# A scheme of 33 products for the last output stage of a cross-attention kernel

## The chip, the cores and the metric

The kernel runs on one core of a Trainium2 chip. Its engines work side by side, each on its own queue of instructions: PE (TensorE, matrix products), DVE (VectorE), ACT (ScalarE), POOL (GpSimd) and SP (SyncE, which here issues the transfers). They wait for each other on semaphores. The metric is the time of one execution on the device in microseconds (us); it is the median of several runs.

## The reference

Two batches of 2048 tokens with 640 channels attend, with 20 heads of 32 channels, to two short contexts of 77 tokens each (a text and an image prompt), which have their own softmax. Everything is in float32. Cut to what matters:

```
q = heads(x @ Wq.T)
k, v = heads(text @ Wk.T), heads(text @ Wv.T)
k_ip, v_ip = heads(ip @ Wk_ip.T), heads(ip @ Wv_ip.T)
out = softmax(q k^T / sqrt(32)) v + softmax(q k_ip^T / sqrt(32)) v_ip
return out @ Wo.T + bo + x
```

The change lies in the last line, for the second batch: a 640x640 matrix times 640x2048 attention outputs, plus a bias and the residual x.

## The kernel before, in words

All matrices lie with the channels on the 128 partitions, so 640 channels are five chunks (`NC = 5`). A step `u` is one chunk of four heads for half of a batch's tokens (1024): there are 20 steps. A step makes queries (PE, line 221), scores (L253), takes them out of the PSUM banks (ACT, L265), forms maxima, differences, exponentials, sums and quotients (DVE L274 and L292, POOL L279 and L299, ACT L285), transposes the result (DVE L306) and multiplies it with the values (PE L315); ACT copies the attention output into `aT` (L338 and L342). The order in which each engine's queue holds these pieces is written out by hand, step by step, in the table `ORDERS`; the output products of the first batch are put between the pieces of steps 10 to 19 (`OUTPUT`).

The output is formed for token blocks of 512. For the first four channel chunks, inputs and outputs both, a block is a 2x2 matrix of blocks (two pairs of chunks, two halves of 256 tokens), and seven products stand for the eight that it needs (Strassen's scheme in Winograd's form). `sum_t` forms differences of token blocks on POOL (L414), `sum_w` differences of weights (L384, once, on POOL), `product` runs on PE (L481 over the first four chunks, L491 for the fifth one, which rides along in four of the seven products), and `take_product` adds the banks to the residual on DVE (L506 with the bias, L512 without). The fifth output chunk is a plain product, `last_chunk` (L461), taken by `store_last` (L471).

For the second batch the four token blocks are done in a tail, after the loop. Near the end of the loop (step 19) SP loads the residual tokens from HBM again: `begin` issues three pieces of the last chunk and the first block (L844 to L848), and after the loop come the last piece and three more blocks. Then stand the 16 differences on POOL, and the list of 28 products and four last chunks in the order in which PE takes them. Inside a block a product writes a bank, is added to the residual, and joins the next product's sum in the same bank where the scheme shares it (`JOINS`). Finished parts are stored at once.

What the tail reads: `aT` (attention outputs), `wo` (Wo, within the tile `wo_ct`), the differences of weights in the fourth x tile, `xs[3]`. The differences of tokens lie in the first three x tiles and in `pb`, the tile that held the probabilities; the residual lies in `pb`, `acc` and `res`.

Of the kernel before, what the change touches and what calls it, by code (L numbers as in the profile page):

```python
# [1 line left out]

# [8 lines left out]
ALU = mybir.AluOpType  # L11
AX = mybir.AxisListType

B, S, C, CC, LT = 2, 2048, 640, 1024, 154
H, D, TEXT = 20, 32, 77
# [4 lines left out]
def kernel(  # L20
# [25 lines left out]
    nc = tc.nc  # L46
    P = 128
    NC = C // P
    NCC = CC // P
    G = P // D  # L50
    TB = 512
    NH = 2
    BLK = NH * TB
    NT = BLK // P
    SUB = S // BLK
    NHB = SUB * NH
    GROUPS = ((0, 3), (3, 3), (6, 2))
    L = TEXT
    assert TEXT == IP and SUB == 2
    NK = (2 * L + D - 1) // D  # L60
    LP = NK * D
    SCALE = 1.0 / float(D) ** 0.5
    NP = B * NC
    NU = NP * SUB
    OPEN = 4
# [7 lines left out]
    banks = [psum.tile([P, TB], F32, name=f"bank_{n}") for n in range(2 * G)]  # L73
    halves = banks[:G], banks[G:]
    wqs = [const.tile([P, NC, P], F32, name=f"wq_{n}") for n in range(3)]
    bo_sb = const.tile([P, NC], F32, name="bo_sb")
    kT = const.tile([P, NC, B, 2, L], F32, name="kT")
    v4s = [const.tile([P, G, NK, D], F32, name=f"v4_{n}") for n in range(2)]
    xs = [const.tile([P, NC, TB], F32, name=f"x_{n}") for n in range(NHB)]
    aT = const.tile([P, (NC + 1) * NHB, TB], F32, name="aT")  # L80

    acc = const.tile([P, NC - 1, TB], F32, name="acc")
    res = const.tile([P, TB], F32, name="res")
# [11 lines left out]
    wo = wo_ct.rearrange("p (k o) -> p k o", k=NC)  # L95
# [95 lines left out]
    XROOM = NHB - 1  # L191
# [131 lines left out]
    def rows_of_attention(b, c):  # L323


        if b == 0:
            return aT[:, ts(c + 1, NHB)]
        if c == 0:
            return aT[:, ts(0, NHB)]
        return aT[:, NHB + c - 1 : NHB + NHB * NHB : NHB]  # L330
# [23 lines left out]
    a11, a12, a21, a22 = wide[:, 0, 0], wide[:, 1, 0], wide[:, 0, 1], wide[:, 1, 1]  # L354
# [31 lines left out]
    def block(b, i, r, h):  # L386

        m, n = (
            4 * (k + 1) + i if b == 0 else 4 * i + k + 3 if k else i for k in (r, r + 2)
        )  # L390
        return aT[:, m : n + 1 : n - m, ts(h, HT)]

    pb_flat = pb.rearrange("p z n g l -> p (z n g l)")
    pb_tiles = pb_flat.rearrange("p (n t) -> p n t", t=TB)

    def t_of(m, b, i):


        raw = {1: (0, 0), 2: (1, 0), 3: (1, 1)}
        if m in raw:  # L400
            return block(b, i, *raw[m])
        if b == 0:
            return t1_room if m == 5 else block(b, i, *{6: (0, 0), 7: (0, 1), 4: (1, 0)}[m])
        sums = pb_tiles[:, : NC - 1] if i == XROOM else xs[i][:, : NC - 1]
        return sums[:, (5, 7, 6, 4).index(m)].rearrange("p (kp t) -> p kp t", kp=2)

    def sum_t(m, b, i):
        x, y = {
            5: (block(b, i, 0, 1), block(b, i, 0, 0)),
            7: (block(b, i, 1, 1), block(b, i, 0, 1)),  # L410
            6: (block(b, i, 1, 1), t_of(5, b, i)),
            4: (block(b, i, 1, 0), t_of(6, b, i)),
        }[m]
        nc.gpsimd.tensor_tensor(t_of(m, b, i), x, y, ALU.subtract)  # L414
# [5 lines left out]
    def sums_of(b, i):  # L420
        if b == 0 or i == 1:
            return acc
        return pb_tiles[:, ds((NC - 1) * (i + 1), NC - 1)]

    def last_of(b, i):
        return res if b == 0 or i == XROOM else xs[i][:, NC - 1]

    def part_in(t, s, h):
        return t.rearrange("p (op s) (h t) -> p s h op t", s=2, h=2)[:, s, h]
# [6 lines left out]
    def in_dram_last(t, b, i):  # L436
        return t[ts(NC - 1, P), ds(b * S + i * TB, TB)]
# [21 lines left out]
    def last_chunk(ps, b, i, ks):  # L459
        for k in ks:  # L460
            nc.tensor.matmul(  # L461
                ps,
                wo[:, k, ts(NC - 1, P)],
                rows_of_attention(b, k)[:, i],
                start=(k == 0),
                stop=(k == NC - 1),
            )

    def store_last(ps, b, i):
        t = last_of(b, i)  # L470
        nc.vector.scalar_tensor_tensor(t, ps, bo_sb[:, NC - 1 :], t, ALU.add, ALU.add)  # L471
        store(b, i, "last")

    def product(m, b, i, ps):


        fifth = {2: (0, 0), 5: (1, 1), 3: (None, 1), 4: (1, 0)}.get(m)
        for op in range(2):
            part = ps[:, ts(op, HT)]
            for kp in range(2):  # L480
                nc.tensor.matmul(  # L481
                    part,
                    w_of[m][:, kp, op],
                    t_of(m, b, i)[:, kp],
                    start=(op == kp == 0 and m in (1, 2, 5)),
                    stop=(op == 1 and kp == 1 and not fifth),
                    skip_group_check=True,
                )
            if fifth:
                s, h = fifth  # L490
                nc.tensor.matmul(  # L491
                    part,
                    w_last[:, op] if s is None else wo[:, NC - 1, ts(2 * op + s, P)],
                    rows_of_attention(b, NC - 1)[:, i, ts(h, HT)],
                    start=False,
                    stop=(op == 1),
                    skip_group_check=True,
                )

    def take_product(m, b, i, ps):  # L500
        part = {2: (0, 0), 1: (0, 0), 5: (1, 1), 7: (1, 1), 3: (0, 1), 6: (0, 1), 4: (1, 0)}[m]
        t = part_in(sums_of(b, i), *part)
        if m in (5, 3, 4, 1 if b else 2):
            for op in range(2):
                bias = bo_sb[:, ds(2 * op + part[0], 1)]
                nc.vector.scalar_tensor_tensor(  # L506
                    t[:, op], ps[:, ts(op, HT)], bias, t[:, op], ALU.add, ALU.add
                )
                if b and m == 4:
                    nc.sync.dma_start(out=in_dram(outT, b, i, *part)[:, op], in_=t[:, op])  # L510
        else:
            nc.vector.tensor_tensor(t, t, ps.rearrange("p (op t) -> p op t", op=2), ALU.add)  # L512
        if m in (6, 7, 2 if b else 1) or m == 4 and not b:
            store(b, i, part)
# [11 lines left out]
    for k in (0, half):  # L526
        nc.sync.dma_start(
            out=wo_ct[:, ds(k * B * LT, half * B * LT)].rearrange("p (k n) -> p k n", k=half),
            in_=ctxT[ds(k * P, half * P), :].rearrange("(k p) n -> p k n", p=P),
# [16 lines left out]
    for t in range(2):  # L546

        ps = halves[t][G - 2 + t]
# [176 lines left out]
    for u in range(NU + 1):  # L725
        for e, text in enumerate(ORDERS[kind_of(u)][2:]):
            for t in text.split():
                m = u - 1 if t[-1] == "-" else u
                t = t.strip("-")
                if t[0] == "C" and t != "CA":  # L730
                    w = work[(m, int(t[1:]))][0]
# [18 lines left out]
    for t, u in queues[3]:  # L750
        if t[0] == "G":
            m = (None, 5, 6, 7, 4)[int(t[1])]
            i = sum(1 for x in sums_at if x[0] == m)
            sums_at[(m, i)] = (t, u)
            work[(t, u)] = (m, i)
    JOINS = {3: 5, 6: 1, 7: 6, 4: 7}
    for t, u in queues[0]:
        if t[0] == "F":
            n = int(t[1:])
            w = work[(u, n)]  # L760
# [15 lines left out]
    late = [c for c in chunks if c[0] >= SUB * NC]  # L776
    for e in range(4):
        for t, u in queues[e]:
            q, b, c, sub = step_of(u)
            ahead = need.setdefault((t, u), [])  # L780
            k, i = t[0], t[1:]
# [20 lines left out]
            elif k == "C":  # L802
                w = work[(u, int(i))]
                ahead += [("F" + i, u)]
                if w[0] == "q":
                    n = chunks.index(w[1:]) - 5
                    if n >= 0:
                        m, h = chunks[n]
# [3 lines left out]
            elif k == "F":  # L812
                w = work[(u, int(i))]
# [11 lines left out]
            elif k == "G":  # L825
                m, n = work[(t, u)]
# [11 lines left out]
    def begin(u):  # L838

        q, _, _, sub = step_of(u)  # L840
        load_w()
        if sub == 1 and q + 3 < NP:
            load_wq(q + 3)
        if u == NU - 1:  # L844

            for i in range(OPEN - 1):
                nc.sync.dma_start(out=last_of(1, i), in_=in_dram_last(xT, 1, i))
            fetch_sums(0)  # L848

    def fetch_sums(i):  # L850
        nc.sync.dma_start(
            out=sums_of(1, i),
            in_=xT[: (NC - 1) * P, ds(S + i * TB, TB)].rearrange("(o p) t -> p o t", p=P),
        )

    def emit(t, u):
        q, b, c, sub = step_of(u)
# [51 lines left out]
    while any(queues):  # L909
# [4 lines left out]
                written.add(queue.pop(0))  # L914
                moved = True
        assert moved, [queue[:1] for queue in queues]
    nc.sync.dma_start(out=last_of(1, XROOM), in_=in_dram_last(xT, 1, XROOM))
    for i in range(1, NHB):
        fetch_sums(i)
    for i in range(NHB):  # L920
        for m in (5, 7, 6, 4):
            sum_t(m, 1, i)
    ends = [held[("p", i)] for i in range(OPEN)]
    free = [p for p in banks if all(p is not t for t in ends)] + ends
    at = {}
    for m, i in (
        (1, 0), ("o", 0), ("o", 1), ("o", 2), ("o", 3), (2, 0), (5, 0), (1, 1), (2, 1), (5, 1),
        (3, 0), (6, 0), (3, 1), (6, 1), (7, 0), (1, 2), (7, 1), (2, 2), (4, 0), (5, 2), (4, 1),
        (1, 3), (2, 3), (5, 3), (3, 2), (6, 2), (3, 3), (6, 3), (7, 2), (7, 3), (4, 2), (4, 3),
    ):  # L930
        if m == "o":
            last_chunk(ends[i], 1, i, (NC - 1,))
            store_last(ends[i], 1, i)
            continue
        at[(m, i)] = at.pop((JOINS[m], i)) if m in JOINS else free.pop(0)
        product(m, 1, i, at[(m, i)])
        take_product(m, 1, i, at[(m, i)])
        if m in (2, 3, 4):
            free.append(at.pop((m, i)))


# [1 line left out]
_TOKENS = ("x", "ctx_2048")  # L943
# [28 lines left out]
```

## Time and profile before

| what | us |
|---|---|
| median of 3 runs | 508.86 (508.68 to 509.0) |
| span of the profiled execution | 506.7 |
| between that span and the median of the runs | 2.16 |
| busy in the span: PE | 498.3 (98%) |
| busy in the span: DVE | 391.9 (77%) |
| busy in the span: POOL | 395.0 (78%) |
| busy in the span: ACT | 242.5 (48%) |
| the tail's first product on PE starts | 437.12 |
| its last DVE instruction ends | 503.88 |

The page gives a span for the profiled execution, from its first instruction to its last; the time of a run is longer by what lies around it. The table's difference is taken between that span and the median. Engines overlap, so their busy times do not add up to the span. In a group of instructions "128x512" is partitions by elements, and the mean is the duration of one instruction. A matrix product in float32 leaves two records on PE. In the order of time, a bracket gives the idle time ahead of an instruction and what ended it.

### The profile page before, as it was taken

What the parts mean: (1) busy time and instruction counts of PE and PEld (TensorE: products, weight loads), DVE (VectorE), ACT (ScalarE), POOL (GpSimd) and SP (SyncE); (2) the same over time, 40 slices, a digit from 0 to 9 for tenths busy, and PEclk for the clock granted to TensorE, in tenths of its full rate; (3) what the DMA queues carried; (4) which work ended last, traced back from release to release, by engine and by line L of the source; (5) the groups of instructions that cost most, each with busy time, mean ns of one, the idle gap of its engine ahead of it and who ended that gap; (6) DMA issues with size and microseconds to landing.
All of it is one profiled execution on the core that took longest, in us unless ns stands there. A gap on an engine that the chain in (4) does not pass through costs nothing.

```text
span 506.7 us, 10153 instructions
## 1 busy us (share of the span) xinstructions
PE 498.3 (98%) x4270; PEld 321.0 (63%) x4270; DVE 391.9 (77%) x347; ACT 242.5 (48%) x423; POOL 395.0 (78%) x163
## 2 busy tenths in 40 slices
PE   9999999999999999999999999999999999999997
PEld 5657557557656565456565656554755775588885
DVE  0079999999899987958997997699899999333333
ACT  1266666666676566645545636454654750100000
POOL 0079999989989988899999997798899999940000
PEclk9999999999999999999999999999999999999999
DMA  8982621331362453885574485168323242641213
GB/s 274 357 210 61 159 69 46 86 92 46 92 185 74 112 198 116 284 314 145 159 237 124 131 260 158 53 178 292 110 72 95 86 162 65 225 147 62 84 41 104
DMA packets 71053, 73.03 MB, mean 144 GB/s; under 512 B 5600, under 2 KB 50912, under 8 KB 71008
## 3 DMA queue, kind: packets, MB, share of 16 engines
q1 hardware_dynamic: 70288, 71.67, 45.9%
q8 instruction: 33, 0.54, 0.5%
q10 hardware_dynamic: 720, 0.72, 0.4%
q14 instruction: 12, 0.10, 0.1%
HBM read 58.61 MB, written 10.49 MB: 136 GB/s over the span
## 4 chain that ended last, share of the span: by engine, by line
PE 86%; DMA 5%; POOL 4%; DVE 1%; SPq 1%; issue 1%; ACT 0%; DVEq 0%; POOLq 0%
PE bank L221 31%; PE bank L481 18%; PE bank L253 9%; PE bank L315 9%; PE bank L137 9%; PE bank L461 5%; PE bank L491 5%; DMA x<-in_x_dram 3%; DMA wo_ct<-in_L_xattn_Wo_dram 2%; POOL pb L299 2%; POOL pb L279 1%; SPq L175 1%; POOL x L384 1%; DMA acc<-in_x_dram 1%; PE bank L541 1%
## 5 line engine op out<-in xcount | busy, mean ns | idle before, releaser
L279 POOL TENSOR_TENSOR pb<-pb,mx 128x1848 f32<-128x1848 f32 (+1 forms) x60 | 175.4, 2941 | 45.3 <-DVE mx L274 45.1
L221 PE MATMUL bank<-x,wq 128*128 128x512 f32 x400 | 180.7, 601 | 0.1
L299 POOL TENSOR_TENSOR pb<-pb,rden 128x1848 f32<-128x1848 f32 (+1 forms) x60 | 175.0, 2939 | 5.2 <-DVE rden L294 5.2
L274 DVE TENSOR_REDUCE mx<-pb 128x24 f32<-128x1848 f32 (+1 forms) x60 | 109.6, 1845 | 33.0 <-ACT pb L265 32.8
L265 ACT COPY pb<-bank 128x462 f32<-128x462 f32 (+1 forms) x240 | 101.7, 535 | 59.3 <-PE bank L253 58.5
L221 PEld LDWEIGHTS bank<-x,wq 128*128 128x128 f32 x400 | 74.1, 191 | 85.0 <-issue 81.7
L292 DVE TENSOR_REDUCE den<-pb 128x24 f32<-128x1848 f32 (+1 forms) x60 | 110.4, 1840 | 17.3 <-ACT pb L285 16.9
L285 ACT ACTIVATE pb<-pb 128x1848 f32<-128x1848 f32 (+1 forms) x60 | 94.9, 1582 | 56.4 <-POOL pb L279 56.2
L306 DVE STREAM_TRANSPOSE pb<-pb 128x1920 f32<-128x1920 f32 (+1 forms) x60 | 114.8, 1923 | 2.1 <-POOL pb L299 2.1
L253 PEld LDWEIGHTS bank<-kT,qT 32*128 32x128 f32 x1280 | 47.4, 184 | 26.3 <-issue 18.0
L253 PE MATMUL bank<-kT,qT 32*128 32x154 f32 x1280 | 58.7, 306 | 0.7 <-ACT vT L899 0.4
L315 PE MATMUL bank<-pb,v 32*32 32x512 f32 x1600 | 55.8, 597 | 1.2 <-ACT pb L265 0.7
L481 PE MATMUL bank<-aT,wo_ct 128*128 128x256 f32 x192 | 47.6, 382 | 1.0 <-DVE acc L512 0.7
L137 PEld LDWEIGHTS bank<-wo_ct,aT 128*128 128x128 f32 x320 | 43.1, 188 | 4.2 <-issue 3.5
L315 PEld LDWEIGHTS bank<-pb,v 32*32 32x32 f32 x1600 | 30.7, 103 | 23.2 <-issue 11.8
L137 PE MATMUL bank<-wo_ct,aT 128*128 128x154 f32 x320 | 45.3, 295 | 0.0
L481 PEld LDWEIGHTS bank<-aT,wo_ct 128*128 128x128 f32 x192 | 36.0, 190 | 11.0 <-issue 3.8
L231 ACT COPY qT<-bank 128x512 f32<-128x512 f32 x40 | 23.1, 588 | 31.4 <-PE bank L221 31.4
L461 PE MATMUL bank<-aT,wo_ct 128*128 128x512 f32 x80 | 36.1, 597 | 0.0
L506 DVE SCALAR_TENSOR_TENSOR pb<-bank,bo_sb,pb 128x256 f32<-128x256 f32 x24 | 10.5, 479 | 26.9 <-PE bank L491 16.4
L491 PE MATMUL bank<-aT,wo_ct 128*128 128x256 f32 x96 | 28.6, 379 | 0.0
L506 DVE SCALAR_TENSOR_TENSOR acc<-bank,bo_sb,acc 128x256 f32<-128x256 f32 x40 | 17.0, 466 | 13.3 <-PE bank L491 6.6
(47 smaller groups left out, 286.2 us busy)
## 6 DMA issues: line engine op xcount, KB each, us to landing
x<-in_x_dram SPq DMA_DIRECT2D x20, 1280.0 KB, 6.9
x<-in_x_dram SPq DMA_DIRECT2D x21, 256.0 KB, 5.2
out_dram<-acc SPq DMA_DIRECT2D x19, 256.0 KB, 2.8
acc<-in_x_dram SPq DMA_DIRECT2D x16, 256.0 KB, 6.7
v<-vS SPq DMA_DIRECT2D x160, 20.0 KB, 1.8
pb<-in_x_dram SPq DMA_DIRECT2D x3, 1024.0 KB, 7.6
wq<-in_L_xattn_Wq_dram SPq DMA_DIRECT2D x9, 320.0 KB, 4.8
aT<-in_L_xattn_Wk_dram SPq DMA_DIRECT2D x5, 512.0 KB, 5.6
```

Of the source, the lines that this page charges most:

```text
L137: nc.tensor.matmul(keys_in(out), loaded[n][:, k, :], cT[:, k, :, t, :], start=(k == 0), stop=(k == NCC - 1))
L221: nc.tensor.matmul(pq, wqs[q % 3][:, k, :], xs[place_of(u, h)][:, k, :], start=(k == 0), stop=(k == NC - 1),)
L253: nc.tensor.matmul(ps[g][:, ts(t, 2 * L)], qTs[(u, h)][g * D : (g + 1) * D, ts(st, P)], kT[g * D : (g + 1) * D, c, b].rearrange("p t l -> ...
L265: nc.scalar.copy(keys_of(u, s)[:, :, g], ps[g][:, : n * 2 * L].rearrange("p (n l) -> p n l", n=n))
L274: nc.vector.tensor_reduce(mx, rows_of(u, s), AX.X, ALU.max)
L279: nc.gpsimd.tensor_tensor(rows_of(u, s), rows_of(u, s), maxs[s].unsqueeze(3).to_broadcast([P, n, 2, L]), ALU.subtract)
L285: nc.scalar.activation(e, e, AF.Exp, scale=SCALE)
L292: nc.vector.tensor_reduce(den, rows_of(u, s), AX.X, ALU.add)
L299: nc.gpsimd.tensor_tensor(rows_of(u, s), rows_of(u, s), rdens[s].unsqueeze(3).to_broadcast([P, n, 2, L]), ALU.mult)
L306: nc.vector.transpose(p, p)
L315: nc.tensor.matmul(pa[r][g * D : (g + 1) * D, :], v4s[q % 2][rows, g, k, :], zones[rows, :, g, k, :], start=(k == 0), stop=(k == NK - 1),)
L481: nc.tensor.matmul(part, w_of[m][:, kp, op], t_of(m, b, i)[:, kp], start=(op == kp == 0 and m in (1, 2, 5)), stop=(op == 1 and kp == 1 and ...
```

## The change

The second batch's tail is written anew; the first batch's output and all of the attention stay.

The first four output chunks by all five input chunks are now one 4x5 matrix of 128x128 weight blocks, and the 2048 tokens' attention outputs a 5x2 matrix of blocks with 1024 tokens each. A scheme of 33 products stands for the 40 that this needs. Each product is one block of weights (raw, or a sum) times one block of tokens (raw, or a sum), and runs twice, once for each 512 columns.

- `W_SUMS`: 25 sums of 128x128 weight blocks, 40 instructions on DVE, into `pb`. 37 of them stand in DVE's queue ahead of the first evacuation of a bank.
- `R_SUMS`: 25 sums of token blocks, 128x1024. 20 are on POOL, five (L, G, J, X and P) on DVE, at given places in its queue. They go to `xs[3]`, free parts of `aT` and `pb`, and three of them over attention outputs that nobody needs any more.
- `CHAINS`: the products are added up in eight chains; each chain has one bank for a token half, and after each stage the bank as it then stands is added to or taken from some outputs. That gives 62 additions on DVE, and four for the last output chunk, all 128x512.
- `TAIL` gives the order in which all of these are issued. A later product of a chain waits until DVE has read the bank of the stage before.
- The residuals are no longer loaded again, but for one block: the x tiles still hold the tokens of the last three query blocks, and sums are formed in them in place. The fourth block is loaded after the loop, into `acc` and `res`.
- One of the four parts of Wo (`a21`) was overwritten in the first batch's scheme. Two transfers load it again after the loop, and SP issues them behind the first batch's last store.

The diff, cut to its core:

```diff
         if sub == 1 and q + 3 < NP:
             load_wq(q + 3)
-        if u == NU - 1:
-
-            for i in range(OPEN - 1):
-                nc.sync.dma_start(out=last_of(1, i), in_=in_dram_last(xT, 1, i))
-            fetch_sums(0)
...
-    nc.sync.dma_start(out=last_of(1, XROOM), in_=in_dram_last(xT, 1, XROOM))
-    for i in range(1, NHB):
-        fetch_sums(i)
...
-    for i in range(NHB):
-        for m in (5, 7, 6, 4):
-            sum_t(m, 1, i)
...
-        product(m, 1, i, at[(m, i)])
-        take_product(m, 1, i, at[(m, i)])
...
+    PRODUCTS = (
+        "01 11, 03 Q, K C, M 00, 30 E, B M, L 30, 31 S, W 40, D X, "
...
+    TAIL = (
+        "xpA.0 wG wP wU wQ wV wX wW wC wD wA wI wJ wT wE wO m31.1.0 wH wF m31.0.1 wN wM o2 wK wS m0.0.1 wL q2 "
+        "xpS.1 m25.0.2 t0.0.11 m0.1.0 t6.0.10 m25.1.3 t0.1.11 xpU.2 m7.1.6 t6.1.10 o1 t2.1.21 o3 t2.1.31 "
...
+    for kp in range(2):
+        nc.sync.dma_start(
+            out=a21[:, kp],
+            in_=WoT[ts(2 * kp, P), : (NC - 1) * P].rearrange("p (op s o) -> p s op o", s=2, o=P)[:, 1],
+        )
+    nc.sync.dma_start(
+        out=acc,
+        in_=xT[: (NC - 1) * P, ds(S + fourth * TB, TB)].rearrange("(o p) t -> p o t", p=P),
+    )
+    nc.sync.dma_start(out=res, in_=xT[ts(NC - 1, P), ds(S + fourth * TB, TB)])
...
+    def add_part(o, ps, op):
+        t = sum_at(o)
+        if o in untouched:
+            untouched.discard(o)
+            nc.vector.scalar_tensor_tensor(t, t, bo_sb[:, o[0] : o[0] + 1], ps, ALU.add, op)
+        else:
+            nc.vector.tensor_tensor(t, t, ps, op)
+        parts_left[o] -= 1
+        if not parts_left[o]:
+            m, i = o
+            nc.sync.dma_start(out=outT[ts(m, P), ds(S + i * TB, TB)], in_=t)
...
+    for word in TAIL:
+        k, rest_ = word[0], word[1:]
+        if k == "w":
+            out = weight(rest_)
+            (op, a), *more = terms(W_SUMS[number(rest_)])
...
+            for n, (o2, b) in enumerate(more):
+                if n == 0 and op == ALU.subtract:
+                    nc.vector.scalar_tensor_tensor(out, weight(a), -1.0, weight(b), ALU.mult, o2)
+                else:
+                    nc.vector.tensor_tensor(out, weight(a) if n == 0 else out, weight(b), o2)
+        elif k == "x":
+            e, (w, where) = rest_[0], rest_[1:].split(".")
...
+            (nc.vector if e == "d" else nc.gpsimd).tensor_tensor(places[w], ra, rb, op)
...
+            nc.tensor.matmul(ps, weight(w), tokens_of(x)[:, h], start=first, stop=True, skip_group_check=True)
```

In `TAIL`, w is a sum of weights, xp a token sum on POOL and xd one on DVE, m a product (number, token half, bank), t an addition of a chain's bank to an output, o a last chunk on PE and q its addition.

## The prediction

> **What bounds the kernel now.** I read first the page's busy shares and its 40 slices, to see which engine is never free and where that changes. Columns of the slices: 12.7 us each, busy tenths.
>
> ```profile
> PE 498.3 (98%) x4270; PEld 321.0 (63%) x4270; DVE 391.9 (77%) x347; ACT 242.5 (48%) x423; POOL 395.0 (78%) x163
> ...
> PE   9999999999999999999999999999999999999997
> ...
> DVE  0079999999899987958997997699899999333333
> ...
> POOL 0079999989989988899999997798899999940000
> ```
>
> PE is full to the end. DVE and POOL are nearly full until slice 34; in the last six DVE has two thirds of its time to spare, and from about 449 us POOL has nothing to do. The change lies there. Next the stretches of ten us (columns: engine busy us with instruction counts, granted clock, DMA share, GB/s), and the instructions of PE, POOL and DVE in order of time (start, duration, group).
>
> ```profile
> 420.00:430.00 10.00, 10.00 (x31) 5.62 (x30) 9.93 (x10) 0.37 (x1) 9.97 (x5) 1.00 0.24 76
> 430.00:440.00 10.00, 9.66 (x175) 5.29 (x174) 1.39 (x3) 2.31 (x8) 9.84 (x8) 1.00 0.54 156
> 440.00:450.00 10.00, 10.00 (x42) 7.67 (x41) 5.03 (x10) 0.00 (x0) 8.78 (x8) 1.00 0.79 296
> 450.00:460.00 10.00, 10.00 (x48) 8.81 (x47) 3.54 (x8) 0.00 (x0) 0.00 (x0) 1.00 0.08 26
> ```
> ```profile
> 437.12 1.99 PE L481 MATMUL bank<-aT,wo_ct 128*128 128x256 f32 x8 [0.34 <-ACT aT L342]
> 438.95 3.60 PE L461 MATMUL bank<-aT,wo_ct 128*128 128x512 f32 x8
> 442.38 1.03 PE L481 MATMUL bank<-aT,wo_ct 128*128 128x256 f32 x4
> ...
> 502.38 0.59 PE L491 MATMUL bank<-aT,wo_ct 128*128 128x256 f32 x2
> ```
> ```profile
> 427.04 3.56 DVE L306 STREAM_TRANSPOSE pb<-pb 128x1920 f32<-128x1920 f32 x2
> ...
> 503.01 0.87 DVE L506 SCALAR_TENSOR_TENSOR pb<-bank,bo_sb,pb 128x256 f32<-128x256 f32 x2 [1.71 <-PE bank L491]
> ```
> ```profile
> 428.73 2.49 POOL L414 TENSOR_TENSOR x<-aT 128x512 f32<-128x512 f32 x2
> ```
>
> The tail begins at 437.12, when ACT has emptied the first bank of the last attention, and PE ends at 502.38 + 0.59 = 502.97 without a gap: 65.85 us, bound by PE at full clock (1.00). DVE ends at 503.88, the span at 506.7, 2.8 later (a store). A matmul is two records: four of 512 columns take 442.38 - 438.95 = 3.43, so 0.86 each, and one of 256 takes 0.43. The prices come from the groups with shapes apart (busy, mean ns) and the DMA issues (KB, us to landing):
>
> ```profile
> L512 DVE TENSOR_TENSOR acc<-acc,bank 128x512 f32<-128x512 f32 x15 | 9.9, 657 | 3.6 <-PE bank L481 2.0 <-PE bank L491 1.7
> L471 DVE SCALAR_TENSOR_TENSOR res<-bank,bo_sb,res 128x512 f32<-128x512 f32 x5 | 3.5, 702 | 0.1
> L384 POOL TENSOR_TENSOR x<-wo_ct 128x256 f32<-128x256 f32 x1 | 0.7, 742 | 0.0
> L539 DVE MEMSET pb<- 128x128 f32 x1 | 0.2, 165 | 0.8 <-PEq L955 0.8
> ```
> ```profile
> out_dram<-pb SPq DMA_DIRECT2D x9, 256.0 KB, 2.2
> ...
> acc<-in_x_dram SPq DMA_DIRECT2D x1, 1024.0 KB, 6.1
> ...
> out_dram<-pb SPq DMA_DIRECT2D x6, 128.0 KB, 1.8
> ```
>
> **The change, part by part.**
>
> *PE.* Removed: 28 products, per token block four of six matmuls and three of four, 4 x 36 = 144 of 256 columns, 144 x 0.43 = 62.1 us. Added: 33 products for two token halves, 66 of 512 columns, 66 x 0.8625 = 56.9. The four last-chunk matmuls (3.45) stay. PE's tail falls from 65.6 to 60.4, by 5.2. Its first product needs the same freed bank and one POOL sum done by 431.1, so it starts at 437.12 and, if never held, ends at 497.5. Weight loads stay covered: 190 ns against a pass of 430 now, 215 before.
>
> *End.* One DVE sum of 512 (0.66) in place of a pair (0.87), but the last store is 256 KB, not 128: 2.2 against 1.8. Together +0.2 to +0.4 after PE's earlier end; I take +0.3. DVE would end at 498.2 instead of 503.88: 5.7 less, 5.4 with the store.
>
> *DVE.* Bank evacuations of batch 1: 66 of 128x512, 20 first ones at 0.71, 46 at 0.66, 44.6 us. New: 40 sums of weights, 128x128, both operands in SBUF. No row has the form; the ends are the memset, 0.165, and the 128x256 evacuation (L506, 466 ns) less 128 elements at the 0.92 ns by which L471 exceeds it, 0.35. With the 0.06 by which neighbours overlap (a pair of 0.47 lasts 0.88) and about a third that wait for the sum before, I take 0.27 from start to start. New too: five sums of 128x1024, 0.66 + 512 x 1.04 = 1.2 each (1.04 ns an element is the slope of the transposes, 1480 ns at 1280 and 2145 at 1920; 1.0 to 1.4). Total 44.6 + 10.8 + 6.0 = 61.4, between about 431 and 498: some 5 us of slack, so DVE's volume alone does not bind.
>
> *POOL.* Removed: 16 sums of 128x512 at 1.27, 20 us, wholly beside PE. Added: 20 of 128x1024; from 742 ns at 256 and 1269 at 512 (L384, L414) the line gives 2.33 each (1.9 by the flatter line of the 1848 and 1232 rows, 3285 and 2250 ns), 46.6 us, from 428.73 to 475 if never held; the last is wanted by the last product near 496. Volume does not bind either.
>
> *DMA and SP.* Gone: three residual loads of 256 KB and three of 1024 KB, four of them in step 19. PE was full there (10.00 of 10) and had to wait for none, so nothing is won and nothing lost; ahead of the tail only these loads differ in the two orders of instructions. New: two 128 KB reloads of a weight block, behind the store issued at 427.14, so issued about 427.6; between 1.8 (20 KB row) and 6.7 (256 KB row) to land, 429.4 to 434.7; I take 431 to 432, near the 64 KB rows (3.6 to 3.9). The first product's own weight lies in that block, and all weight sums wait for both loads; behind these on DVE stands every evacuation. Landing at 434.7 would bring the 23rd weight sum (product 25) to 440.9 against 440.6, so up to then the load costs at most 0.3. The 1024 KB load, 429.4 + 6.1, lands 9 us before its first use.
>
> *What no row shows.* Every DVE instruction that runs beside POOL in this trace reads at most one tensor from SBUF, and POOL keeps 3.28 us per 1848 sum all the while. Now 45 DVE sums read two, while POOL reads two. The ends: they run freely, 0, or each waits for a POOL sum, up to 2.33. I take an exclusion, because POOL's price already hangs on its operands: 2.09 ns an element from 256 to 512 with two full tensors, 1.68 from 1232 to 1848 with a broadcast one. POOL is short of reading, and a second reader is the nearest thing to that.
>
> [...]
>
> With exclusion, the question is who goes next. DVE's neighbours overlap, so a run of its sums leaves gaps only at dependent ones; I take it that DVE's runs go through and POOL waits. Then: POOL does two sums, 428.7 to 433.4 (the second starts before the weights land). DVE's run of 37 weight sums follows, 37 x 0.27 = 10.0, to 443.4, then the first evacuation, 444.1. PE has seven matmuls that need no evacuation, to 437.12 + 7 x 0.8625 = 443.2; it restarts at about 444.4: 1.3 lost. Between 443 and 496 two products wait for large DVE sums that may meet a POOL sum just begun (L before product 23, X before product 9), half of 2.33 each: 2.0 with rounding down for cover. Sum: 503.5 + 1.3 + 2.0 = 506.8.
>
> **The rivals.**
>
> *No conflict.* For it: single-operand DVE work shows none. Against: the form is new. PE runs without a gap: 508.86 - 5.4 = 503.5.
>
> *Turn by turn (slower).* After each weight sum one POOL sum gets in. Product 25 needs the 23rd weight sum by 440.6. First sum 433.4, POOL to 436.1, then nine while POOL waits for ACT (438.7), then four POOL sums with a weight sum each, 4 x 2.6, to 449.2, then nine, to 451.6: PE stands 11.0 us. With the 1.3 for evacuations behind the other 14, and the 2.0: 503.5 + 14.3 = 517.8. It decides from the second POOL sum let in: 2 x 2.33 less 1.0 of slack (433.4 + 23 x 0.27 = 439.6), and 2.0, is 5.7, over the 5.4 won. If POOL's run also shuts DVE out later, it is more, 520 to 530. For it: POOL's neighbours overlap too (2.49 for two of 1.27).
>
> *DVE as the bound.* At 0.35 a weight sum and 1.4 a large one DVE has 65.6 us of work, the run takes 13 us, and evacuations start at 446.4: 3 us more than forecast, 509.8. Inside the forecast's own range, nearly.
>
> **How the numbers follow.** The sums are changes of the profiled execution: its span is 506.7, and 2.16 lies between that and the median of the runs, 508.86; I carry this over, so 506.8 stands for a span of 504.6. Chances: runs of DVE go through 0.52 (own range 505.0 to 509.8), no conflict 0.15, turn by turn or worse 0.33. The range goes from 503.3 to 520, which leaves out what is beyond 520 and little below. 0.2% is 1.0 us, about what a measurement tells from no change: faster is below 507.8. Of the 0.52 I give 0.37 to faster, 0.11 to no change, 0.04 to slower. Faster 0.52, same 0.11, slower 0.37.
>
> **What the profile after would show.** PE: 66 + 4 matmuls of 0.86 in the tail, 60.4 us busy; the first at 437.1. POOL: 20 sums; with exclusion the third starts only near 443 and lasts longer than 2.33 where DVE's sums stand in its time. Without it, POOL's second to fourth follow ACT's copies and PE has no gap. Turn by turn: weight sums 2.6 us apart, and PE idle for 8 to 11 us ahead of product 25. Wrong altogether if PE's gaps lie after 450 in other products, if a weight sum costs over 0.4, or if the reload lands after 435.

## The result, and the profile after

The changed kernel takes 517.26 us (517.18 to 517.36, four runs) against 508.93 before (508.68 to 510.99, four runs), 1.0154 times as long (95% interval 1.0136 to 1.0172). The forecast was 506.8 and faster; the time lies within the range given, at the price of the rival called turn by turn, 517.8.

The page's slices of the changed kernel, 12.9 us each:

```profile
PE 496.8 (96%) x4114; PEld 291.7 (57%) x4114; DVE 441.2 (86%) x410; ACT 242.5 (47%) x423; POOL 424.1 (82%) x167
...
PE   9999999999999999999999999999999999399997
...
DVE  0079999899999979949998997798989999999886
...
POOL 0089999999899888799999979799899998705990
PEclk9999999999999999999999999999999999789999
```

PE has one hole, in slice 35 (438 to 451), and its granted clock falls there and just behind (0.78 and 0.71 in the stretches below). DVE has little time to spare in the tail now. The stretches of ten us show how deep the hole is (engine busy us with counts; then granted clock):

```profile
430.00:440.00 10.00, 9.62 (x171) 4.51 (x170) 9.48 (x15) 2.31 (x8) 7.33 (x4) 1.00 0.46 150
440.00:450.00 10.00, 1.29 (x4) 0.22 (x2) 9.93 (x11) 0.00 (x0) 8.56 (x4) 0.78 0.00 0
450.00:460.00 10.00, 10.00 (x17) 4.37 (x18) 9.74 (x24) 0.00 (x0) 0.00 (x0) 0.71 0.12 44
460.00:470.00 10.00, 10.00 (x24) 4.38 (x24) 8.93 (x15) 0.00 (x0) 2.99 (x2) 1.00 0.12 44
```

In 440 to 450 PE works 1.3 us. DVE is "busy" 9.93 us with 11 instructions, 0.9 us each, where a weight sum should take 0.28. The order of time tells why; first PE, then DVE, then POOL, in the changed kernel:

```profile
440.24 1.02 PE L1064 MATMUL bank<-aT,wo_ct 128*128 128x512 f32 x2
449.97 2.07 PE L1064 MATMUL bank<-aT,pb 128*128 128x512 f32 x2 [8.71 <-DVE pb L1044]
451.84 1.91 PE L1064 MATMUL bank<-aT,wo_ct 128*128 128x512 f32 x2
453.54 1.91 PE L1064 MATMUL bank<-aT,pb 128*128 128x512 f32 x2
455.25 1.31 PE L1064 MATMUL bank<-x,wo_ct 128*128 128x512 f32 x2
456.39 1.88 PE L462 MATMUL bank<-aT,wo_ct 128*128 128x512 f32 x4
```
```profile
431.27 2.77 DVE L1044 TENSOR_TENSOR pb<-wo_ct 128x128 f32<-128x128 f32 x2 [0.25 <-DMA wo_ct<-in_L_xattn_Wo_dram]
434.07 2.36 DVE L1044 TENSOR_TENSOR pb<-pb,wo_ct 128x128 f32<-128x128 f32 x1
436.35 0.28 DVE L1042 SCALAR_TENSOR_TENSOR pb<-pb,wo_ct 128x128 f32<-128x128 f32 x1
...
438.25 3.29 DVE L1044 TENSOR_TENSOR pb<-pb,wo_ct 128x128 f32<-128x128 f32 x4
441.47 2.42 DVE L1044 TENSOR_TENSOR pb<-wo_ct,pb 128x128 f32<-128x128 f32 x1
443.92 2.31 DVE L1044 TENSOR_TENSOR pb<-pb,wo_ct 128x128 f32<-128x128 f32 x1
446.16 2.83 DVE L1044 TENSOR_TENSOR pb<-wo_ct 128x128 f32<-128x128 f32 x3
448.91 0.28 DVE L1044 TENSOR_TENSOR pb<-pb,wo_ct 128x128 f32<-128x128 f32 x1
```
```profile
429.15 4.74 POOL L1050 TENSOR_TENSOR x<-aT 128x1024 f32<-128x1024 f32 x2
433.85 2.43 POOL L1050 TENSOR_TENSOR aT<-aT 128x1024 f32<-128x1024 f32 x1
438.95 2.45 POOL L1050 TENSOR_TENSOR aT<-aT 128x1024 f32<-128x1024 f32 x1 [2.67 <-ACT aT L343]
441.36 4.73 POOL L1050 TENSOR_TENSOR pb<-aT 128x1024 f32<-128x1024 f32 x2
446.17 2.47 POOL L1050 TENSOR_TENSOR pb<-pb,aT 128x1024 f32<-128x1024 f32 x1
467.01 2.36 POOL L1050 TENSOR_TENSOR pb<-aT,pb 128x1024 f32<-128x1024 f32 x1 [18.38 <-DVE pb L1050]
```

A weight sum lasts either 0.28 or about 2.4 us, nothing between. Six of the first 37 are long (one each within the groups at 431.27, 438.25 and 446.16, and the three alone), and six POOL sums run in that time after the first. Each long one ends within 0.2 us of the end of a POOL sum; the profile counts the time that it is held as busy (9.93 of the ten us from 440). There are no more than six because POOL has no more to do: its next sum needs a large DVE sum that stands behind the run (the wait of 18.38 us). From 436.3 to 438.9 POOL waits for ACT, and DVE's sums go by at 0.28. The run of 37 lasts from 431.27 to 453.36, 22.1 us. PE, whose product 25 needs the 23rd, stands 8.71 us, and then three matmuls last 1.87, 1.70 and 1.71 us from start to start in place of 0.86.

### The profile page after: what moved, and what is told of

It reads as the page before. It is cut to its first block, busy times and chain, and to the rows that moved or that the text cites. A ratio compares the mean times of both kernels' runs of the same rounds, so it can differ in the third digit from the quotient of the medians.

```text
span 515.4 us, 9899 instructions
## 1 busy us (share of the span) xinstructions
PE 496.8 (96%) x4114; PEld 291.7 (57%) x4114; DVE 441.2 (86%) x410; ACT 242.5 (47%) x423; POOL 424.1 (82%) x167
## 4 chain that ended last, share of the span: by engine, by line
PE 61%; POOL 14%; DVE 13%; DMA 6%; issue 2%; SPq 1%; ACT 0%; POOLq 0%; DVEq 0%
PE bank L222 25%; PE bank L1064 10%; PE bank L138 9%; PE bank L254 7%; POOL pb L280 7%; PE bank L316 5%; POOL pb L300 5%; DVE pb L1044 3%; PE bank L482 3%; DMA x<-in_x_dram 3%; DVE pb L307 3%; DVE den L293 2%; DMA wo_ct<-in_L_xattn_Wo_dram 2%; DVE mx L275 2%; PE bank L462 1%
## 5 line engine op out<-in xcount | busy, mean ns | idle before, releaser
L1064 PE MATMUL bank<-aT,pb 128*128 128x512 f32 x52 | 26.5, 631 | 8.7 <-DVE pb L1044 8.7
L482 PE MATMUL bank<-aT,wo_ct 128*128 128x256 f32 x128 | 32.0, 383 | 1.1 <-DVE acc L513 1.1
L482 PEld LDWEIGHTS bank<-aT,wo_ct 128*128 128x128 f32 x128 | 23.9, 190 | 8.2 <-issue 3.4
L1025 DVE TENSOR_TENSOR x<-x,bank 128x512 f32<-128x512 f32 x36 | 23.8, 683 | 4.4 <-PE bank L1064 4.1
L462 PEld LDWEIGHTS bank<-aT,wo_ct 128*128 128x128 f32 x80 | 14.9, 190 | 17.4 <-issue 16.6
```

The source lines that it names most:

```text
L1064: nc.tensor.matmul(ps, weight(w), tokens_of(x)[:, h], start=first, stop=True, skip_group_check=True)
```

## The experiments

The theory: while POOL sums two tensors, a DVE instruction with two tensors in SBUF waits for the whole POOL sum; behind it the next POOL sum goes first, so one weight sum passes for each POOL sum, and every evacuation stands behind the run. Rivals: the run is long by itself (the form, the late reload, DVE's volume); any DVE instruction collides; the engines share in proportion; the slow clock is what costs. The diffs are cut to the lines that act.

**POOL behind the run (e1_gate).**

```diff
             places[w] = place_for(where)
+            if w == "S":
+                nc.gpsimd.tensor_copy(gate_sb, weight("L")[:, :1])
```

> One short POOL copy of the last weight sum stands ahead of POOL's second token sum, so POOL's sums come behind DVE's run of 37 weight sums. Turn by turn (each weight sum waits for one POOL sum): with no POOL sum in the way, the run takes 37 x 0.28 = 10.4 us, to 441.7, no weight sum is longer than 0.4, PE's gap ahead of product 25 (8.7 us) is gone, product 7 waits about 1 us, and the time is 507.3 (505.5 to 509). Rival, the run is long by itself (the form, the late reload of the weight block, DVE's volume): the weight sums take as long as before, POOL is only later, 517 or more.

506.93 us, 0.9966 of before (0.9953 to 0.9979). In the order of time, POOL waits 9.35 us at the copy, and DVE's first and last weight sums of the run and PE's product 25 stand so:

```profile
440.56 0.18 POOL L1052 COPY gate_sb<-pb 128x1 f32<-128x1 f32 x1 [9.35 <-DVE pb L1045]
```
```profile
430.97 0.58 DVE L1045 TENSOR_TENSOR pb<-wo_ct 128x128 f32<-128x128 f32 x2 [0.25 <-DMA wo_ct<-in_L_xattn_Wo_dram]
...
440.20 0.29 DVE L1045 TENSOR_TENSOR pb<-pb,wo_ct 128x128 f32<-128x128 f32 x1
```
```profile
440.79 1.02 PE L1067 MATMUL bank<-aT,pb 128*128 128x512 f32 x2
```

The same 37 sums take 9.5 us, 430.97 to 440.49, and PE goes on at 440.79 without a gap. The run is not long by itself, and the reload is in time in both kernels. One wait of POOL is worth 10.3 us. PE still pauses at three places, each behind a DVE sum that meets POOL later:

```profile
456.63 1.12 PE L1067 MATMUL bank<-pb 128*128 128x512 f32 x2 [1.09 <-DVE pb L1053]
...
471.77 2.32 PE L1067 MATMUL bank<-pb 128*128 128x512 f32 x4 [0.28 <-DVE pb L1053]
...
489.68 1.13 PE L1067 MATMUL bank<-pb,wo_ct 128*128 128x512 f32 x2 [1.00 <-DVE x L1026]
```

**No POOL sums (e2_no_pool).**

```diff
+            if e == "p":
+                places[w] = ra
+                continue
             places[w] = place_for(where)
-            (nc.vector if e == "d" else nc.gpsimd).tensor_tensor(places[w], ra, rb, op)
+            nc.vector.tensor_tensor(places[w], ra, rb, op)
```

> POOL's 20 token sums are left out; the products read one raw token block in place of each. DVE keeps all its sums and evacuations. Turn by turn: without a POOL sum DVE has its path alone, PE is not held, 503.5 (503 to 504.5): the scheme's own worth. Rival, DVE's volume binds (some 65 us of work from 431): 509 to 510, with DVE full to the end. Rival, the run of weight sums is long by itself: PE stands ahead of product 25 as before, about 517.

503.48 us, 0.9898 of before (0.9882 to 0.9914). With all of DVE's work in place PE is not held, so DVE's volume does not bind; the scheme is worth 5.2 us here, and the other 13.8 us come with POOL's sums. That they come from collisions, and not from products that wait for POOL's sums, is shown by e5_gates below, which keeps all of these sums.

**One operand: transposes (e3_one_operand), and products with a constant (e8_scalar).** Each replaces all 40 weight sums. The fence has one line of what goes and the line that comes, with the run's name behind it.

```diff
-                    nc.vector.tensor_tensor(out, weight(a) if n == 0 else out, weight(b), o2)
+                nc.vector.transpose(out, weight(b))                                   # e3_one_operand
+                nc.vector.tensor_scalar(out, weight(b), -1.0, None, ALU.mult)         # e8_scalar
```

> Each of the 40 weight sums is replaced by a transpose of 32x32 blocks of the same 128x128 elements, which reads one tensor from SBUF and writes the same place; the weights are therefore not the scheme's. POOL does all its sums. If the second SBUF operand is what collides: the 37 take about 0.28 each beside POOL, PE has no gap ahead of product 25, only the five large DVE sums still meet POOL's, 504 to 506. Rival, any DVE instruction that reads or writes SBUF waits for POOL's sum: 517.

> Each of the 40 weight sums is replaced by a product of one raw block with -1, which reads one tensor from SBUF and writes SBUF; the weights are therefore not the scheme's. If only a second tensor from SBUF collides, none is held by POOL, and the time is that of the transposes, 505.6 (504.5 to 506.5). [...]

The transposes: 505.61 us (0.9933 of before, 0.9916 to 0.995). The products with -1: 514.33 (1.0099, 1.0083 to 1.0115). 34 of the 40 instructions of the line (the other six last at most 0.273 and 0.220 us), with least, median and longest duration in ns, for the transposes and then for the products:

```profile
L1039 DVE STREAM_TRANSPOSE pb<-wo_ct x34: 269/307/314, 430.3 to 452.7; 128x128 f32<-128x128 f32 x34
```
```profile
L1039 DVE TENSOR_SCALAR pb<-wo_ct x34: 214/227/2408, 431.4 to 462.9; 128x128 f32<-128x128 f32 x34
```

No transpose lasts over 0.314 us beside the same POOL sums: it is not any DVE instruction that collides. A product with a constant does: it takes 0.21 when free, under the median of 0.28 to 0.29 of a sum, and six take up to 2.4. It reads one tensor, so a second operand is not needed; the expectation that named only that was too narrow. What sums and products share, and transposes lack, no run here shows.

**Half the POOL sum (e6_half).**

```diff
+                for h in range(NH):
+                    nc.gpsimd.tensor_tensor(places[w][:, h], ra[:, h], rb[:, h], op)
```

> Each POOL token sum is issued as two of 128x512. If one DVE sum waits for one POOL instruction, whatever its length: 12 long weight sums in place of six, about 1.3 us in place of 2.4, and nearly the same time, 517 (516 to 518.5). Rival, the two engines share a path in proportion (a DVE sum beside POOL is slowed by a fixed part): the number and length of the long sums stay as they were, six of 2.4.

515.12 us (1.0105 of before, 1.0083 to 1.0128), 0.9 below the expected range. Weight sums of this kernel, and its sums X and P:

```profile
L1044 DVE TENSOR_TENSOR pb<-pb,wo_ct x20: 279/291/1345, 433.3 to 465.5; 128x128 f32<-128x128 f32 x20
L1044 DVE TENSOR_TENSOR pb<-wo_ct x9: 281/532/1360, 431.4 to 451.6; 128x128 f32<-128x128 f32 x9
L1051 DVE TENSOR_TENSOR pb<-pb,aT x2: 1433/1724/2015, 479.7 to 496.0; 128x1024 f32<-128x1024 f32 x2
```

The longest is now 1.36, the length of one POOL instruction of 512 columns (1.26) and a little, and 12 are long in place of six. So a held instruction waited for one POOL instruction, at both lengths tried (2.4 beside sums of 2.36, 1.36 beside halves of 1.26); sharing in proportion would have left six of 2.4. PE's hole stays, 8.66 us. The gain I had not counted lies later: X and P, two of the large DVE sums, last at most 2.0 in place of 2.8 and 3.1, and the two pauses of PE behind them are gone.

**PE kept busy in the hole (e4_pe_busy).**

```diff
+            if (m, h) == (25, 0):
+                for _ in range(10):
+                    nc.tensor.matmul(ps, weight("10"), tokens_of("11")[:, 0], start=True, stop=True, skip_group_check=True)
```

> Ten extra products of raw blocks (8.6 us) run in product 25's bank ahead of it, in the time in which PE stands for its weight sum; product 25 starts the bank anew. If PE's slow matmuls from 450 to 455.5 (1.7 us in place of 0.86) come from the granted clock after the gap: they run at 0.86 and the time falls by 2.5 to 2.9, to 514.6. Rival, they wait for evacuations: unchanged, 517, or longer by what the extra products overrun.

516.7 us, 1.0156 of before (1.0139 to 1.0174), where the changed kernel stood at 1.0154: not 2.5 to 2.9 us less, but 0.6 by the medians and nothing by the ratios, which is within the noise. In the order of time:

```profile
441.02 8.75 PE L1065 MATMUL bank<-aT,wo_ct 128*128 128x512 f32 x20
449.94 1.12 PE L1067 MATMUL bank<-aT,pb 128*128 128x512 f32 x2 [0.17 <-DVE pb L1044]
450.90 1.02 PE L1067 MATMUL bank<-aT,wo_ct 128*128 128x512 f32 x2
451.76 1.02 PE L1067 MATMUL bank<-aT,pb 128*128 128x512 f32 x2
454.14 1.10 PE L1067 MATMUL bank<-x,wo_ct 128*128 128x512 f32 x2 [1.36 <-DVE x L1023]
```

The clock is full (1.00 in 440 to 450 and in 450 to 460), the matmuls take 0.86, and PE then stands 1.36 us for the first evacuation (453.25), which still waits behind the 14 other weight sums. The slow clock was real, but it lay almost wholly within waits for evacuations that were there anyway.

**The gate after the 23rd weight sum (e7_gate_T).**

```diff
+            if w == "S":
+                nc.gpsimd.tensor_copy(gate_sb, weight("T")[:, :1])
```

> POOL's second token sum waits for the 23rd weight sum (product 25's) in place of the 37th. If the loss is the wait of product 25 for that sum: it is gone, and the time is 507 to 509. If the loss is that all evacuations stand behind the run of 37, however product 25 fares: product 25 starts in time, six of the last 14 weight sums last 2.4 us, PE stands ahead of product 7 and after it, and the time is 516 to 517.5.

517.0 us (1.0155 of before, 1.0136 to 1.0173): nothing won.

```profile
436.50 2.33 DVE L1045 TENSOR_TENSOR pb<-pb,wo_ct 128x128 f32<-128x128 f32 x1
438.75 2.43 DVE L1045 TENSOR_TENSOR pb<-wo_ct,pb 128x128 f32<-128x128 f32 x1
441.11 2.43 DVE L1045 TENSOR_TENSOR pb<-wo_ct 128x128 f32<-128x128 f32 x1
443.46 2.42 DVE L1043 SCALAR_TENSOR_TENSOR pb<-wo_ct 128x128 f32<-128x128 f32 x1
```
```profile
441.55 1.02 PE L1067 MATMUL bank<-aT,pb 128*128 128x512 f32 x2
452.84 2.04 PE L1067 MATMUL bank<-x,wo_ct 128*128 128x512 f32 x2 [10.27 <-DVE x L1024]
```

Product 25 comes in time, the six collisions fall on the last 14 sums, and PE stands 10.27 us ahead of product 7 for the first evacuation. So what the run costs here is set by when its last sum ends, and not by product 25's own weights: everything that frees a bank stands behind it.

**All collisions of weight (e5_gates).**

```diff
+            behind = {"S": weight("L"), "W": weight("B"), "D": places.get("X"), "R": places.get("P")}.get(w)
+            if e == "p" and behind is not None:
+                nc.gpsimd.tensor_copy(gate_sb, behind[:, :1] if len(behind.shape) == 2 else behind[:, 0, :1])
```

> Four short POOL copies: POOL's second token sum waits for DVE's 37th weight sum, its seventh for the last weight sums ahead of L, its twelfth for X and its eighteenth for P. Turn by turn: beside the gap of the weight sums, the later collisions go too, where a DVE sum of 1024 lasted 2.8 to 3.1 us in place of 1.2 and PE lost 1 us each behind it: 505.2 (504 to 506.5), all large DVE sums at 1.2 to 1.9. Rival, PE's remaining gaps come from the order of the evacuations and not from collisions: 507, as with the first gate alone.

503.58 us, 0.989 of before (0.9875 to 0.9905), 1.6 less than expected and 0.1 from the kernel without POOL's sums. X and P, the token sums on DVE, in the changed kernel (L1050 there); then G and J, X and P, and a pause of PE in this one:

```profile
L1050 DVE TENSOR_TENSOR pb<-pb,aT x2: 2775/2952/3128, 479.5 to 496.5; 128x1024 f32<-128x1024 f32 x2
```
```profile
L1054 DVE TENSOR_TENSOR pb<-aT x2: 1210/2210/3209, 459.1 to 462.2; 128x1024 f32<-128x1024 f32 x2
L1054 DVE TENSOR_TENSOR pb<-pb,aT x2: 1218/1218/1218, 467.8 to 484.1; 128x1024 f32<-128x1024 f32 x2
462.36 3.12 PE L1068 MATMUL bank<-pb 128*128 128x512 f32 x6 [0.47 <-DVE pb L1054]
```

X and P are at 1.22. One sum still meets POOL (G, 3.21), and PE stands 0.47 us for it, its only pause past the first product. This kernel beats both, by 5.2 and 13.7 us.

## Why the prediction was wrong

- **The mechanism and its place: right.** No row of before had a DVE instruction with two SBUF tensors beside POOL; the prediction took an exclusion from POOL's price by operands, and it is there (weight sums of 0.28 that last 2.4 beside POOL's). The argument from that price was the author's estimate, and that POOL is short of reading, no run shows; the runs show the exclusion.
- **The step that failed** is "DVE's neighbours overlap, so a run of its sums leaves gaps only at dependent ones; I take it that DVE's runs go through and POOL waits". POOL did not wait for the end of a run: one weight sum passed, and the next POOL sum went, six times over (6 x 2.1 = 12.6 us, the difference of the two runs, 22.1 and 9.5). POOL's neighbours overlap just as closely, as the rival said (two of 2.37 last 4.69 in e1_gate, so by 0.05, where the prediction has 0.06 for DVE's); the row spoke for neither side, and I let it decide.
- **The price of what was assumed: right in sum, by luck in its parts.** Where POOL is made to wait (e1_gate), the time is 506.93, against 506.8. But there POOL's second sum waits too, so the run starts at 430.97 and not at 433.4, and the 1.3 us ahead of the first evacuation are not lost: PE has no pause from 437.28 to 455.5. Three later collisions cost some 3.3 us of PE (1.25 at L, where a weight sum ahead of it is held for 2.1, then 0.9 at X and 1.2 at P), where the sum had two at 2.0 together.
- **The rival, turn by turn: right but for its parts.** 517.8 against 517.26. It had PE stand 11.0 us ahead of product 25 and 1.3 for evacuations; measured are 8.71, and 3.0 over the next nine matmuls (10.7 us for 7.7). Its point of decision, the second POOL sum let in, was not tried. It named product 25 as the place; the gate after the 23rd sum shows that a hold among the last 14 does as well.
- **The terms.** The scheme without conflict: 503.5 forecast, 503.48 with POOL's sums left out. A matmul of 0.86, PE starting near 437.1 (437.59 in this profile), the reload landing near 431.2, a weight sum 0.27 (37 in 9.5 us, 0.26), a large DVE sum 1.2 (1.22), a POOL sum 2.33 (2.36): all held. (POOL's 2.09 ns an element is 2.06 from the rows named, 742 and 1269; nothing rests on the difference.) The two later collisions, L and X at 2.0 together, were of the right kind; by the changed kernel's trace they were X and P, 0.6 and 1.1 us of PE.
- **Not forecast:** the clock's fall (0.50 from 450 to 455.3), which cost some 0.6 us or nothing that can be told from noise.

## What to carry to other kernels

When DVE work moves beside POOL work, count the operands in SBUF, and do not take a single operand for safe: beside POOL's sums of two tensors, sums of two (0.28 when free) lasted up to 2.4 us, the products with -1, of one tensor (0.21 when free), up to 2.4 too, and the transposes, also of one, at most 0.314. A short DVE instruction that collided cost here not its own time but one POOL instruction (2.36, or 1.26 when halved); the run of 37 short ones cost six of those, as many as POOL had ready, together with all that stands behind them in DVE's queue. A schedule that assumes an order between the two engines needs a dependency that enforces it: four short copies on POOL's queue were worth 13.7 us. And price a run by what stands behind its last instruction, not by the first one that somebody waits for.

## What the runs showed that I had not expected

- The two engines took turns instruction by instruction even where both had their next one ready: in e7_gate_T five weight sums in a row, from 436.50 to 448.23, lasted 2.31 to 2.43 each, while POOL did five sums, from 436.27 to 448.08. Neither went through with a run. With POOL's instructions at half length, 12 DVE sums were held in place of six.
- Time in which a DVE instruction was held is told as its busy time, so the profile shows no wait at all: 0.28 and 2.4 us for one shape are the only sign. POOL shows it too: in the changed kernel a sum of 2.36 lasts 3.35 where X or P came first, and in e5_gates one of the copies of one column 1.05 in place of 0.18.
- After PE's gap of 8.7 us three matmuls took about twice their time (1.70 to 1.87 for 0.86), 5.3 us together, and the granted clock was 0.50 from 450 to 455.3. With PE kept busy (e4_pe_busy) it did not occur: the clock was 1.00 in 440 to 450 and in 450 to 460.
